# A chain of selective scans on one core: the softplus sum moved to TensorE, and three of sixteen products moved to GpSimd

## The chip, the core and the metric

The kernel runs on one core of a Trainium2 chip. The metric is the device time of one execution in microseconds, the median of several runs. Engines are named as in the profile: PE (TensorE), DVE (VectorE), ACT (ScalarE), POOL (GpSimd), and SP, which issues all the DMA.

## The reference

Four images of 64 x 64 positions with 96 channels pass through four layers. Layer 0 has a gated recurrence; layers 1 to 3 have a two-dimensional selective scan. Every layer ends in a feed-forward block with quantized operands. In layers 1 to 3 the image is normalised, projected to 192 inner channels and a gate z, convolved 3 x 3, and scanned in four orders (rows, columns, each forward and backward), with 16 states per channel. Cut to what matters, from the reference:

```python
dt = jax.nn.softplus(delta + delta_bias[None, :, None])
dA = jnp.exp(dt4[..., None] * A4[None, :, :, None, :])
dBu = dt4[..., None] * u4[..., None] * Bt[:, :, None, :, :]
def step(h, ab):
    a, b = ab
    h = a * h + b
    return (h, h)
_, hs = jax.lax.scan(step, h0, (dA_l, dBu_l))
y = jnp.einsum('lbkdn,lbkn->lbkd', hs, C_l)
return y + u * Dskip[None, :, None]
```

B and C are rows over positions for each state n, the same for all channels. The four orders are added, normalised, multiplied by silu(z) and projected back.

## The kernel before

Layer 0 runs first (`gated`). Then `scans` goes through 12 stages: 4 images for each of layers 1, 2 and 3. A stage has 24 items: 2 directions x 4 segments of T = 1024 positions x 3 chunks of 128 (channel, order) pairs. An item has 16 tiles, one for each state n. That makes 4608 tiles of 128 partitions x 1024 positions in fp32.

For one tile the work is:

- `c_rows`: two DMAs spread the row of C over 64 partitions each, from a scratch tensor `cs` in DRAM (4 buffers).
- `decays`: ACT computes da = exp(delta x decay), into SBUF (3 buffers).
- `b_rows`: PE spreads the row of B over the partitions with a selection matrix `sel`, two bf16 matmuls of 512 columns into a PSUM tile `bc` (2 buffers).
- `scan`: DVE multiplies bc by du = delta x u in place, then runs the scan h = da h + bc.
- `carry`: ACT copies the last column of h for the next segment.
- `times_c`: POOL multiplies h by the rows of C, in place (h has 4 buffers).
- `accumulate`: PE adds h into a PSUM accumulator with four fp32 quarter matmuls. fp32 matmuls are two instructions each in the trace.

The order is written by hand, and each engine works strictly in the order in which its instructions are written (`InOrder`). The loop over k writes, in step k: `carry(k-1)`, `c_rows(k+2)`, `decays(k+2)`, `b_rows(k+1)`, `scan(k)`, `times_c(k-1)`, then side work, then `accumulate(k-2)`.

Side work is written as generators (`Chain`), each `yield` being a point at which the loop takes over again; `pump` advances a chain to its next yield. `yield True` asks for a free PSUM bank, of which side work has two. There are three kinds:

- `prepare_chunk` makes delta and du for the next item. Softplus is computed as max(x, 0) + log(1 + e) with e = exp(-|x|), plus a correction term for the rounding of 1 + e. ACT computes the terms, and POOL adds them in three passes over 128 x 1024. It is pumped once a step and drained at n = 13. Its Ln needs an ACT table other than that of Exp; `logarithms()` uses the visit for the pending norms, and is called once more at n = 11.
- `next_segment` loads u and projects it to the rows of B, C and delta.
- `Job(between(...))` is everything between two layers of another image: joining the four orders, the output projection (`mixer_out`), the feed-forward block, then normalisation, the input projection and the convolution (`convolve`) for the next layer. `Job.step` pumps all its chains `rate` times a step: 1.4, and 1.9 for the last layer's ends. At step 356 of a stage what is left of the job is finished at once. The last image's end runs after the last scan.

All instructions are recorded by one helper, so the profile puts them all on line L80; tiles tell them apart. In the profile `bc` is the row of B or the product, `h` the state, `da` the decay, `c` the row of C, `cs` the scratch with C, `acc` the accumulator, `e`, `delta` and `du` the softplus and its products.

Of the kernel before, what the change touches and what calls it, by code (L numbers as in the profile page):

```python
# [34 lines left out]


CHUNKS = (((0, 0), (64, 1)), ((0, 1), (64, 0)), ((128, 0), (128, 1)))
# [3 lines left out]
NC3 = 48  # L41
XPW = NB3 + 2 * R + NC3
# [59 lines left out]
def metaformer(ctx: ExitStack, tc: tile.TileContext, x, l0_ab, l0_rest, ssm, ffn, out):  # L102
# [58 lines left out]
    stacked = const("stacked", [128, 64])  # L161
    dve.tensor_copy(stacked[0:64], ident[0:64, 0:64])
    dve.tensor_copy(stacked[64:128], ident[64:128, 64:128])
    twice = const("twice", [128, 128])
    dve.tensor_copy(twice[:, 0:64], stacked)
    dve.tensor_copy(twice[:, 64:128], stacked)
# [5 lines left out]
    sel = const("sel", [NB3, NS, 192], BF16)  # L172
    for n in range(NS):
        for k in range(3):
            at = NS * (k % 2) + n
            dve.tensor_copy(
                sel[:, n, 64 * k : 64 * k + 64], mod32[:, at : at + 1].to_broadcast([NB3, 64])
            )
# [7 lines left out]
    minus = const("minus", [128, 1])  # L186
    pool.memset(minus, -1.0)
# [21 lines left out]
    def moments(src, width):  # L209

        st = sb(5, "st", [128, G, 6])
        mv = sb(5, "mv", [128, G, 2])
        for g in range(G):
            dve.bn_stats(st[:, g, :], src[:, g, 0:width])
        for g in range(G):
            dve.bn_aggr(mv[:, g, :], st[:, g, :])
        return mv

    class Norm:
# [7 lines left out]
        def measure(self, src, width, e):  # L227

            mv = moments(src, width)
            yield  # L230
            act.activation(self.v, mv[:, :, 1], AF.Identity, bias=small[e])
            act.activation(self.nm, mv[:, :, 0], AF.Copy, scale=-1.0)
            pending.append(self)

        def settle(self):

            act.activation(self.r, self.r, AF.Exp, scale=-0.5)
            yield
            refine(self.r, self.v)
            pool.tensor_tensor(self.nm, self.nm, self.r, ALU.mult)  # L240

# [76 lines left out]
    def join_orders(im, s, hold):  # L318

        yr, yc = hold["in"].pop(s)  # L320
        if s + 1 < NSTRIP:
            load_y(im, s + 1, hold)
        cols_a, part_c = hold["cols"]
        yt = sb(2, "yt", [128, G, DI])

        def join(ps, g):

            t0, r0 = 128 * g, SR * s + 2 * g
            o, hi = ps[:, g % 2, 0:128], ps[:, g % 2, 128:DI]
            pe.matmul(o, yr[:, t0 : t0 + 128], ident, start=True, stop=False)  # L330
            for r in range(2):
                v = cols_a.rearrange("p (c r) -> p r c", r=HW)[:, r0 + r, :]
                pe.matmul(o[64 * r : 64 * r + 64], v, ident, start=False, stop=True)
            yield
            pe.matmul(hi, yc[:, t0 : t0 + 128], ident[0:64, 0:64], start=True, stop=False)
            for r in range(2):
                for k in range(2):
                    p = slice(64 * k, 64 * k + 64)
                    v = part_c.rearrange("p (c r) -> p r c", r=HW)[p, r0 + r, :]
                    q = 64 * r + 32 * k  # L340
                    pe.matmul(
                        hi[q : q + 32], v, ident[p, p], start=False, stop=True, tile_position=(64 * k, q)
                    )

        for pair in range(2):
            ps = bank("y_t")[:, 0 : 2 * DI].rearrange("p (g c) -> p g c", g=2)
            yield from join(ps, 2 * pair)
            yield
            yield from join(ps, 2 * pair + 1)
            yield  # L350
            act.copy(yt[:, 2 * pair : 2 * pair + 2, :], ps)
            release()
            yield pair == 0
        norm = Norm()
        yield from norm.measure(yt, DI, 1e-5)
        hold["y", s] = yt, norm

    def mixer_out(im, layer, s, hold):
# [6 lines left out]
        normalise(yt, yt, DI, norm.r, norm.nm)  # L365
        yield True
        g = []
        for i, (a, b, z) in enumerate(((0, 128, zl), (128, 192, zh))):
# [12 lines left out]
            for v, z, m in ((g[0], zl, 128), (g[1], zh, 64)):  # L381
                pool.tensor_tensor(v[0:m], v[0:m], z[0:m], ALU.mult)
                yield m == 64
        ps = bank("out_proj")
        for q in range(G):
# [4 lines left out]
            yield  # L390
        x1 = sb(2, "x1", [128, G, C])
# [12 lines left out]
    def load_y(im, s, hold):  # L404
# [4 lines left out]
        sp.dma_start(out=yr[64:128], in_=im.y[1, 64:128, t])  # L409
# [18 lines left out]
    def feed_forward(im, layer, s, hold, dst):  # L428
# [6 lines left out]
        normalise(xh, x1, C, norm.r, norm.nm)  # L435
        yield True
        ps = bank("ff_xt")
        transpose_strip(ps, xh, 0, C)
        yield
# [18 lines left out]
        pool.tensor_copy(hq[:, 2, :], late, saturate=False)  # L458
        yield True
# [16 lines left out]
        for g in range(G):  # L476
            pool.tensor_tensor(y[:, g, :], y[:, g, :], b[:, 3 : 3 + C], ALU.add)
        yield
        x2 = sb(1, "x2", [128, G, C])
        pool.tensor_tensor(x2, x1, y, ALU.add)  # L480
        yield
        sp.dma_start(out=tokens(dst, s), in_=x2)
        if layer < 3:
            norm = hold["norm", s] = Norm()
            yield from norm.measure(x2, C, 1e-6)
# [74 lines left out]
    def convolve(im, layer, s, hold):  # L560
# [10 lines left out]
        for i, group in enumerate(groups):  # L571
# [8 lines left out]
            raw.append(v)  # L580
        for i, v in enumerate(raw):
            act.activation(v, v, AF.Silu, bias=w[:, W_CB + i : W_CB + i + 1])
# [6 lines left out]
        sp.dma_start(out=im.u[1, 64:128, t], in_=raw[0][64:128])  # L589
# [12 lines left out]
        if s == NSTRIP - 1:  # L602
            yield
            sp.dma_start(out=im.u[1, 0:64, :], in_=cols_a[0:64])
# [7 lines left out]
    def between(im, layer, dst=None):  # L612
# [8 lines left out]
        def first():  # L621
            if layer:
                cols_a, part_c = hold["cols"] = columns()
                sp.dma_start(out=cols_a[0:64], in_=im.y[1, 0:64, :])
# [6 lines left out]
                load_y(im, 0, hold)  # L631
            yield
# [70 lines left out]
    class Job:  # L703
# [7 lines left out]
        def step(self):  # L711
            self.credit = min(self.credit + self.rate, 2.0)
# [33 lines left out]
    def load_segment(item):  # L746
# [8 lines left out]
        sg.cs = dram.tile([NC3, T], F32, tag="cs", name="cs")  # L755
        return sg

    def prepare_segment(item, sg):
# [38 lines left out]
        for k in range(2):  # L797
# [3 lines left out]
            yield from project(ps, m, m + NC3, k)  # L801
            act.copy(sg.rows[0:NC3, cols], ps[0:NC3])
            release()
        sp.dma_start(out=sg.cs, in_=sg.rows[0:NC3])

    def prepare_chunk(item):
# [7 lines left out]
        e = sb(1, "e", [128, T])  # L814
        delta, du = sb(2, "delta", [128, T]), sb(2, "du", [128, T])
        for k in range(2):
            cols = slice(k * MM, (k + 1) * MM)
            ps = bank("dt_proj")
            pe.matmul(ps, f, sg.rows[NB3 : NB3 + 2 * R, cols], start=True, stop=True)
            yield  # L820
            act.activation(e[:, cols], ps, AF.Abs, bias=bias)
            act.activation(delta[:, cols], ps, AF.Relu, bias=bias)
            release()
            yield k == 0
        act.activation(e, e, AF.Exp, scale=-1.0)
        act.activation(du, e, AF.Ln, bias=ones)
        logarithms()
        yield
        pool.tensor_tensor(delta, delta, du, ALU.add)
        yield  # L830
        act.activation(du, e, AF.Identity, bias=ones)
        act.activation(du, du, AF.Identity, bias=minus)
        yield
        yield
        pool.tensor_tensor(e, e, du, ALU.subtract)
        yield
        yield
        yield
        pool.tensor_tensor(delta, delta, e, ALU.add)
        yield  # L840
        yield
# [13 lines left out]
    def scans(stages, jobs, pac):  # L855
# [15 lines left out]
        tiles = [(i, n) for i in items for n in range(NS)]  # L871
        live = {}
# [3 lines left out]
        def c_rows(k):  # L876
            i, n = tiles[k]
            c = live[k, "c"] = sb(4, "c", [128, T])
            for half in range(2):
                row = NS * (CHUNKS[i.chunk][0][1] + half) + n  # L880
                sp.dma_start(
                    out=c[64 * half : 64 * half + 64],
                    in_=i.sg.cs[row : row + 1, :].to_broadcast([64, T]),
                )

        def decays(k):
            i, n = tiles[k]
            da = live[k, "da"] = sb(3, "da", [128, T])
# [3 lines left out]
        def b_rows(k):  # L892
            i, n = tiles[k]
            b = live[k, "b"] = wide()
            swap = CHUNKS[i.chunk][0][1]
            for half in range(2):
                cols = slice(half * MM, (half + 1) * MM)
                pe.matmul(
                    b[:, cols], sel[:, n, 64 * swap : 64 * swap + 128], i.sg.bs[:, cols], start=True, stop=True
                )  # L900

        def scan(k):
# [6 lines left out]
            dve.tensor_tensor(b, i.du, b, ALU.mult)  # L909
# [60 lines left out]
        last = len(tiles) - 1  # L970
        chain = segment = None
        c_rows(0)
# [13 lines left out]
        for k in range(last + 4):  # L986
            q, n = divmod(k, NS)
            if k <= last:
# [16 lines left out]
                if n == 11:  # L1005
                    logarithms()
# [3 lines left out]
            if 0 <= k - 1 <= last:  # L1010
                carry(k - 1)
            if k + 2 <= last:
                c_rows(k + 2)
                decays(k + 2)
            if k + 1 <= last:
                b_rows(k + 1)
            if k <= last:
                scan(k)
            if 0 <= k - 1 <= last:
                times_c(k - 1)  # L1020
            if k >= 3 and (k - 3) % NS == NS - 1:
                store(items[(k - 3) // NS])
            if k <= last:
                pump(chain)
                pump(segment)
                if n == 13:
# [3 lines left out]
                work()  # L1030
            if 0 <= k - 2 <= last:
# [240 lines left out]
    for at in range(len(stages)):  # L1272
        jobs.append([])
        if at + 1 < len(stages):
            im, layer = stages[at + 1]
            jobs[-1].append(Job(between(im, layer - 1), 1.4))

        for im in {10: images[:2], 11: images[2:3]}.get(at, ()):
            jobs[-1].append(Job(between(im, 3, im.dst), 1.9))
# [42 lines left out]
def _scan(in_w, conv_w, conv_b, xp_w, dt_w, dt_b, A_logs, Ds, ln_w, ln_b, out_w):  # L1322
# [5 lines left out]
    for d in range(2):  # L1328
        for chunk, halves in enumerate(CHUNKS):
            for k, (ch, order) in enumerate(halves):  # L1330
# [5 lines left out]
                for s in range(3):  # L1336
                    if s % 2 == order:
                        v[:, m + NS * s : m + NS * s + NS] = t[:, R + NS :]
# [69 lines left out]
```

## Time and profile before

| | us |
|---|---|
| runs | 20164.85, 20133.44, 20149.6 (median 20149.6) |
| profiled execution, device time | 20152.58 |
| its span | 20150.8 |
| layer 0 and start, from the windows view | 0 to 1901 |
| the scans of layers 1 to 3 | 1901 to 19692 |
| end of the last image | 19692 to 20151 |
| DVE busy | 17808.5 |
| PE busy | 16417.6 |
| POOL busy | 15531.3 |
| ACT busy | 12295.0 |

An engine's busy time is the union of its instructions; a "mean ns of one" is the duration of one instruction, and neighbours can overlap by some tens of nanoseconds. "Idle before" sums the time in which the engine stood still just before instructions of the group, and names what ended most of it. Matmuls are pipelined and their ends are modelled. The granted clock of PE is given as a share of full speed.

### The profile page before, as it was taken

To read this page: it belongs to the slowest core of one execution; us is meant where nothing else is said; L and a number is where in the kernel's file an instruction comes from. 1 tells how busy PE (TensorE), PEld (TensorE's weight loads), DVE (VectorE), ACT (ScalarE), POOL (GpSimd) and SP (SyncE) were. 2 spreads that over 40 slices of the span, in tenths; PEclk is the share of its full clock that TensorE was granted. 3 is DMA by queue.
4 is the path that set the end of the run, shared out by engine and by line. 5 is a ranking of instruction groups with operands and counts; after the bars stand their busy time and mean duration, and the time that the engine had idled before them with its cause. 6 is when DMAs were issued, how large, how long until landed. Compare 5 with 4: busy or idle time off the path is not lost. (4 is left out here: it accounts for less than half of the span.)

```text
span 20150.8 us, 220842 instructions
## 1 busy us (share of the span) xinstructions
PE 16417.6 (81%) x70656; PEld 4838.3 (24%) x70656; DVE 17808.5 (88%) x13848; ACT 12295.0 (61%) x19373; POOL 15531.3 (77%) x10470
## 2 busy tenths in 40 slices
PE   8998788787888787788788888788788888887776
PEld 3332121121122222222222222222222222222223
DVE  6665999999999998999999999989999999999881
ACT  4444665665665665665665666666666666666553
POOL 3434888888888887888888888878888888878882
PEclk9898796786887797897887887887887887888775
DMA  0002666666666666666666676666676666676661
GB/s 20 16 18 69 165 181 174 166 186 167 168 184 171 164 179 175 166 182 180 167 187 171 167 189 167 169 180 169 170 187 171 168 187 168 170 188 161 172 169 44
DMA packets 1234532, 3148.68 MB, mean 156 GB/s; under 512 B 428049, under 2 KB 428177, under 8 KB 1227217
## 3 DMA queue, kind: packets, MB, share of 16 engines
q1 hardware_dynamic: 1233360, 3134.55, 58.6%
q8 instruction: 554, 9.08, 0.2%
q14 instruction: 618, 5.05, 0.1%
HBM read 2819.18 MB, written 314.57 MB: 156 GB/s over the span
## 5 line engine op out<-in xcount | busy, mean ns | idle before, releaser
L80 POOL TENSOR_TENSOR h<-h,c 128x1024 f32<-128x1024 f32 x4608 | 10834.6, 2358 | 2827.5 <-ACT carry L80 1727.5
L80 DVE TENSOR_TENSOR_SCAN h<-da,carry,bc 128x1024 f32<-128x1024 f32 x4608 | 10814.5, 2347 | 608.7 <-POOL carry L80 10.3
L80 PE MATMUL acc<-h,stacked 64*64 64x512 f32 x36864 | 6179.1, 747 | 498.7 <-POOL h L80 493.8
L80 ACT ACTIVATE da<-delta,decay 128x1024 f32<-128x1024 f32 x4608 | 5280.9, 1147 | 1648.9 <-DVE h L80 1601.8
L80 DVE TENSOR_TENSOR bc<-du,bc 128x1024 f32<-128x1024 f32 x4608 | 5574.5, 1210 | 611.2 <-PE bc L80 586.0
L80 PE MATMUL bc<-bs,sel 96*128 96x512 bf16 x9216 | 3346.9, 451 | 2071.8 <-DVE h L80 2054.6
L80 ACT COPY carry<-h 128x1 f32<-128x1 f32 x3456 | 649.0, 188 | 3533.7 <-DVE h L80 3529.1
L80 PEld LDWEIGHTS <-sel 96*128 96x128 bf16 x9216 | 551.3, 101 | 6988.6 <-DVE h L80 5085.7
L80 PEld LDWEIGHTS acc<-h,stacked 64*64 64x64 f32 x36864 | 1132.5, 153 | 3286.5 <-issue 1699.7
L80 ACT ACT_TABLE_LOAD x1133 | 1453.6, 1283 | 41.6 <-DVE mv L80 22.5
L80 POOL TENSOR_TENSOR c<-h,c 128x512 f32<-128x512 f32 x384 | 485.7, 1265 | 970.5 <-ACT c L80 614.8
L80 PE MATMUL conv<-pad,tap_lo 128*128 128x512 f32 x1728 | 917.5, 630 | 0.0
L80 PE MATMUL dt_proj<-rows,w 12*128 12x512 f32 x1152 | 828.0, 805 | 0.0
L80 ACT ACTIVATE du<-e,ones 128x1024 f32<-128x1024 f32 x576 | 660.8, 1147 | 228.8 <-POOL delta L80 223.2
L80 PE MATMUL x_proj_b<-u,xp 128*108 128x512 f32 x1152 | 671.9, 699 | 94.3 <-DMA xp<-in_ssm 59.0
L80 ACT ACTIVATE c<-c,l_bias 128x512 f32<-128x512 f32 x384 | 263.5, 686 | 753.0 <-PE c L80 737.9
L80 POOL TENSOR_TENSOR delta<-delta,du 128x1024 f32<-128x1024 f32 x288 | 679.5, 2359 | 12.1 <-ACT du L80 12.1
L80 POOL TENSOR_TENSOR e<-e,du 128x1024 f32<-128x1024 f32 x288 | 679.4, 2359 | 2.4 <-ACT du L80 2.4
L80 POOL TENSOR_TENSOR du<-delta,u 128x1024 f32<-128x1024 f32 x288 | 679.4, 2359 | 0.7
L80 POOL TENSOR_TENSOR delta<-delta,e 128x1024 f32<-128x1024 f32 x288 | 678.5, 2356 | 0.1
L80 PE MATMUL x_proj_c<-u,xp 128*48 128x512 f32 x1152 | 624.3, 655 | 64.3 <-ACT rows L80 64.3
L80 PE MATMUL conv<-pad,tap_hi 128*128 128x512 f32 (+1 forms) x1152 | 638.5, 650 | 8.2 <-ACT u L80 8.2
(155 smaller groups left out, 16118.3 us busy)
## 6 DMA issues: line engine op xcount, KB each, us to landing
c<-cs SPq DMA_DIRECT2D x9216, 256.0 KB, 4.1
u<-u SPq DMA_DIRECT2D x288, 512.0 KB, 7.6
y<-y SPq DMA_DIRECT2D x1152, 128.0 KB, 2.4
y<-y SPq DMA_DIRECT2D x144, 512.0 KB, 5.6
xr<-x SPq DMA_DIRECT2D x224, 192.0 KB, 4.8
u<-u SPq DMA_DIRECT2D x288, 128.0 KB, 4.4
pad<-y SPq DMA_DIRECT2D x288, 128.0 KB, 4.6
z<-zl SPq DMA_DIRECT2D x96, 256.0 KB, 2.0
```

The source lines that it names most:

```text
L80: ins = f(*a, **k).ins
```

## The change

The change has four parts.

1. In `prepare_chunk` softplus is computed half by half (512 columns). ACT makes the four terms, PE adds them in PSUM with four fp32 matmuls by the identity, and ACT copies the sum to delta. The three POOL passes go. The call of `logarithms()` at n = 11 goes.
2. The states 2, 7 and 12 (`ON_POOL`) get their product with B on POOL: two DMAs bring the row of B into an SBUF tile `b` (1 buffer) four steps ahead, POOL multiplies it by du two steps ahead, and DVE runs the scan alone. Their decay goes to one of the two PSUM tiles that the rows of B use, one step ahead instead of two. Their rows of B are stored with C in `cs`.
3. Side work is pumped between the product and the scan of a step instead of after `times_c`, `prepare_chunk` gets a second pump at n = 1, 5, 9 and 13, and many chains get more yields between a step and the one that uses its result. Rates rise to 1.8 and 2.6. The silu of the convolution waits for a step whose second next tile isn't a moved one.
4. The halves of the second chunk are swapped, so that `sel` is smaller and all chunks use one layout; four small additions in `feed_forward` become one.

The core of the diff, without the added yields and the swap:

```diff
+CHUNKS = (((0, 0), (64, 1)), ((64, 0), (0, 1)), ((128, 0), (128, 1)))
+ON_POOL = (2, 7, 12)
...
+            both = sb(1, "e", [128, T])
+            e, rest, log, top = both[:, 0:MM], both[:, MM:T], du[:, cols], delta[:, cols]
...
+            act.activation(e, e, AF.Exp, scale=-1.0)
+            act.activation(log, e, AF.Ln, bias=ones)
+            logarithms()
+            yield
+            act.activation(rest, e, AF.Identity, bias=ones)
+            act.activation(rest, rest, AF.Identity, bias=ones, scale=-1.0)
+            yield True
+            ps = bank("delta")
+            for i, v in enumerate((e, rest, log, top)):
+                pe.matmul(ps, ident, v, start=i == 0, stop=i == 3)
+                if i % 2:
+                    yield
+            act.copy(delta[:, cols], ps)
...
-        pool.tensor_tensor(delta, delta, du, ALU.add)
...
-        pool.tensor_tensor(e, e, du, ALU.subtract)
...
-        pool.tensor_tensor(delta, delta, e, ALU.add)
...
+        def pool_rows(k):
+            i, n = tiles[k]
+            b = live[k, "b"] = sb(1, "b", [128, T])
+            from_rows(i, b, NS + ON_POOL.index(n))
+
+        def times_b(k):
+            i, b = tiles[k][0], live[k, "b"]
+            pool.tensor_tensor(b, i.du, b, ALU.mult)
...
+            da = live[k, "da"] = wide() if on_pool(k) else sb(3, "da", [128, T])
...
+            if not on_pool(k):
+                dve.tensor_tensor(b, i.du, b, ALU.mult)
+            beside()
...
+            def beside():
                 pump(chain)
                 pump(segment)
+                if n % 4 == 1:
+                    pump(chain)
                 if n == 13:
                     drain(chain, work)
                     if item.chunk == 2:
                         drain(segment, work)
                 work()
+            if 0 <= k - 1 <= last:
+                carry(k - 1)
+            if on_pool(k + 1):
+                decays(k + 1)
+            if k + 2 <= last:
+                c_rows(k + 2)
+                if not on_pool(k + 2):
+                    decays(k + 2)
+            if on_pool(k + 4):
+                pool_rows(k + 4)
+            if k + 1 <= last and not on_pool(k + 1):
+                b_rows(k + 1)
+            if 0 <= k - 1 <= last:
+                times_c(k - 1)
+            if on_pool(k + 2):
+                times_b(k + 2)
...
+                scan(k, beside)
...
-            jobs[-1].append(Job(between(im, layer - 1), 1.4))
+            jobs[-1].append(Job(between(im, layer - 1), 1.8))
```

## The prediction

> **What bounds the kernel now.** I read first the page's shares by engine and its costliest groups, then the busy time by stage, then who waited for whom inside the scan stage, then the timeline of single tiles. From the page (engine, operation, tiles, count | busy us, mean ns | idle just before, releaser):
>
> ```profile
> PE 16417.6 (81%) x70656; PEld 4838.3 (24%) x70656; DVE 17808.5 (88%) x13848; ACT 12295.0 (61%) x19373; POOL 15531.3 (77%) x10470
> ...
> L80 POOL TENSOR_TENSOR h<-h,c 128x1024 f32<-128x1024 f32 x4608 | 10834.6, 2358 | 2827.5 <-ACT carry L80 1727.5
> L80 DVE TENSOR_TENSOR_SCAN h<-da,carry,bc 128x1024 f32<-128x1024 f32 x4608 | 10814.5, 2347 | 608.7 <-POOL carry L80 10.3
> ...
> L80 DVE TENSOR_TENSOR bc<-du,bc 128x1024 f32<-128x1024 f32 x4608 | 5574.5, 1210 | 611.2 <-PE bc L80 586.0
> ...
> L80 ACT ACT_TABLE_LOAD x1133 | 1453.6, 1283 | 41.6 <-DVE mv L80 22.5
> ...
> L80 POOL TENSOR_TENSOR delta<-delta,du 128x1024 f32<-128x1024 f32 x288 | 679.5, 2359 | 12.1 <-ACT du L80 12.1
> ```
>
> The scans of layers 1 to 3 run from 1901 to 19692 us. The windows view of that stage (us, then busy us of PE, PEld, DVE, ACT, POOL, granted clock, DMA share, GB/s):
>
> ```profile
> 1901.00:19692.00 17791.00, 14439.66 (x64938) 3986.25 (x64930) 16540.16 (x11838) 11257.85 (x17220) 14714.40 (x8979) 0.81 0.65 174
> ```
>
> DVE is the bound: busy 93%. Of its 1251 us idle, 608 us are 132 ns between each product and its scan; 642 us are real waits, nearly all the product waiting for PE's rows of B (586 us). The timeline shows what a tile costs undisturbed (start us, length us):
>
> ```profile
> 10000.50 2.35 DVE L80 TENSOR_TENSOR_SCAN h<-da,carry,bc 128x1024 f32<-128x1024 f32 x1
> ...
> 10002.76 1.21 DVE L80 TENSOR_TENSOR bc<-du,bc 128x1024 f32<-128x1024 f32 x1
> ...
> 10004.11 2.35 DVE L80 TENSOR_TENSOR_SCAN h<-da,carry,bc 128x1024 f32<-128x1024 f32 x1
> ```
>
> Scan to scan is 3.61 us, and 3604 ns is the median over all 4608 tiles. 4608 x 3.604 = 16,607 us; DVE's side work (statistics, residual adds, remainders) adds 542, the waits 642: 17,791. Outside this stage lie 1901 + 459 us of span and 1.8 us around it: 20,152.6 us for the profiled execution, 3.0 us above the median shown.
>
> **The change, part by part.**
>
> *Product moved (DVE).* 3 of 16 tiles are 864. Each loses 1210 + 132 ns on DVE, its pitch falling from 3604 to 2262 ns: **-1159 us**. The scan then reads b from SBUF and da from PSUM; before it was the reverse, so one operand from each: I keep 2347 ns. No row has this pairing; the two scan shapes (1280 ns for 512 columns in the opening stage, 2347 for 1024) leave 213 ns of fixed cost, and half of that either way bounds it: 92 us.
>
> *Side work between product and scan (DVE).* It can fill the 132 ns: about 900 groups, 0 to -119 us. Often it will itself wait for PE or ACT there: **-40**.
>
> *GpSimd.* It loses three softplus passes an item (288 x 3 x 2359 ns) and gains three products (864 x 2358): zero in sum; its 14,714 us then fill about 87% of a shorter stage. But the place matters: the product for tile k+2 is queued in step k behind times_c(k-1), which waits for scan(k-1) and ACT's carry (0.4 us). It ends 0.4 + 2.36 + 2.36 = 5.1 us after scan(k-1), and scan(k+2) may start after two pitches, 7.2 us (6.9 if a step is short in side work). So 1.9 us of lateness are free. GpSimd's side work (1.27 us for a gate product, 0.61 for a cast, 2.36 for du) exceeds this now and then; what queues behind is times_c, then PE's accumulation. Bounds 0 and 864 x 1 us; I take 0.17 us a tile: **+150**.
>
> *ACT.* An item loses 1044 + 2 x 1147 + 1149 ns of full-width passes, and gains eight half-width ones (about 0.67 us each, the Abs/Relu rows) and two copies (0.57): +2.0 us. Ln is now visited twice an item, each visit two table loads of 1283 ns; the explicit flush at n = 11 goes, so loads rise only from 3.2 to 4 or 5 an item. ACT stays near 75%, but look at one visit now:
>
> ```profile
> 10566.50 1.04 ACT L80 ACTIVATE e<-e 128x1024 f32<-128x1024 f32 x1
> 10567.55 1.28 ACT L80 ACT_TABLE_LOAD   x1
> 10568.85 1.15 ACT L80 ACTIVATE du<-e,ones 128x1024 f32<-128x1024 f32 x1
> 10570.02 1.28 ACT L80 ACT_TABLE_LOAD   x1
> 10571.31 1.15 ACT L80 ACTIVATE da<-delta,decay 128x1024 f32<-128x1024 f32 x1
> ```
>
> It is 4.8 us in a 3.6 us step; the carry behind it is late, then times_c, PE's accumulation, and the next rows of B: at 10577.6 us a pitch of 4.15 follows. By scan starts sorted by state, the pitch after n = 3 averages 4200 ns, of which about 445 are wait: 128 us in all. After the change there are two such visits, the first around n = 1, 2 (with the store's 0.99 us copy and a 2.26 us step), the second around n = 7, 8 (again a short step); PE's sum then waits in order for the last ACT term with the rows of B behind it. Bounds 0 (the added yields absorb it) and 3 us an item (864); I take 0.9 us an item: **+250**. The decay of a moved tile is made one step ahead instead of two, in a PSUM buffer freed by scan(k-1); behind the carry it needs 1.4 of 3.6 us, hidden unless ACT is over 2 us late, which is in these bounds.
>
> *PE.* Gained: 288 x 2 x 4 = 2304 fp32 matmuls of 512 columns, two instructions each. Nearest row: conv with tap_lo, 841.6 us busy for 1584 instructions in this stage, 531 ns each: +2448 us. Lost: 1728 instructions for rows of B at 3343.8/9208 = 363 ns: -627. So PE's busy time goes from 14,440 to 16,261 us, above DVE's own floor of about 15,950. This is the dangerous number. Two rows bear on it, one conv tap at either clock:
>
> ```profile
> 10006.95 1.82 PE L80 MATMUL conv<-pad,tap_lo 128*128 128x512 f32 x2
> ...
> 10016.04 1.02 PE L80 MATMUL conv<-pad,tap_lo 128*128 128x512 f32 x2
> ```
>
> The granted clock in the trace is either 1 or 0.5, 0.81 in the mean here, and it was 0.92 in the convolution stretch of a stage (9987 to 10438 us), where PE is busiest, against 0.73 just after it. Taps back to back start 429 ns apart at full clock; by that, the added work is 1977 us and a busy PE has room. It is tight only in the convolution stretch: side rounds go from 1.4 to 1.8 a step, so per step about 1.2 us of convolution, 1.3 of rows and sums, 0.8 of projections and softplus, 3.3 of 3.45 us. That is some 116 steps in each of 11 stages; 0.15 us each: **+190** (0 to 500).
>
> The Trainium skill (Perfetto Trace Analysis, Identifying the Most-Contended Engine) holds matmul busy time a poor measure, since matmuls are pipelined; by it the 16,261 us bind nothing. By the row alone PE would be the longest engine. The skill (TensorE: Matmul & The Clock Gate, Part 1) says an idle window halves the clock and a busy one restores it; by it the added matmuls raise the mean clock, say to 0.9 (an estimate), and PE's time would be 16,261 x 0.81/0.9 = 14,635 us; with the row's 0.81 kept it stays 16,261. No row settles it.
>
> *Queues and jobs.* SP issues 1728 more 256 KB loads: +453 MB, about 212 GB/s and a DMA share near 0.8 instead of 0.65. They come after the rows of C in SP's order and have about 3.7 us of margin beyond the 4.1 us they take to land; nothing on the path, up to +150 if landing doubles. Added yields are paid by the higher rates (old 1.4 x 18/15 is below 1.8). Convolution strips finish earlier, before the forced finish at step 356, which now stalls the product 18.1, 18.0 and 17.0 us: **-53**. More yields elsewhere move nothing: their cover is DVE's pitch.
>
> Sum: 20,152.6 - 1159 - 40 + 150 + 250 + 190 - 53 = **19,490 us**.
>
> **Rivals.** *All is absorbed:* no new wait, 20,152.6 - 1159 - 119 - 53 = 18,820 to 18,940. For it: POOL and ACT total little more than before. Against: every margin shrinks with the pitch. *PE becomes the bound, still faster:* 16,261 us at the 93% that DVE holds today is 17,485 for the stage, 19,850 in all. For it: 81% busy already, products wait for PE alone. Against: the clock rises with load. *Slower:* the softplus sum blocks PE's queue. It stands before the accumulation and the next rows of B, waits there for ACT's last term, and at half clock its two matmuls take 3.6 us; the rows have some 2.9 us of margin (a pitch, less the 0.6 us that they take). If each of the two visits costs 2.8 us, that is 288 x 5.6 = 1610: 20,152.6 - 1252 + 1610 = 20,510. It decides from 1252/288 = 4.3 us of new wait an item, against 2.2 us of all waits today. For it: today's single visit already shows the chain. Against: at full clock the same two matmuls take half.
>
> **How the numbers follow.** Forecast 0.50, all absorbed 0.12, PE-bound 0.15, slower 0.19, and 0.04 that gains and waits cancel within 0.2%, about what a measurement of this kernel can tell from no change. Faster is 0.50 + 0.12 + 0.15 = 0.77. The range reaches from the absorbed case's upper part, 18,880, to 20,340, below the middle of the slower case; the forecast's own range is 19,000 to 19,900.
>
> **What would show it.** Right: 3744 products on DVE; scan to scan near 2.26 us into a moved tile; mean pitch near 3.71 us; POOL's total unchanged; product waits on PE and scan waits on POOL's b together some 1200 us, against 642; clock above 0.81. Wrong: PE busy over 93% of the stage or clock not above 0.81 (PE-bound); waits of products on PE over 1900 us, bunched after the Ln visits (slower); scans longer than 2.35 us with b in SBUF; DMA landing over 8 us.

## The result, and the profile after

The changed kernel takes **21,415.8 us** (median of four runs, 21,398.0 to 21,433.9) against 20,141.5 for the kernel before beside it (20,123.3 to 20,164.9): a ratio of 1.0632, 95% interval 1.0614 to 1.065. It is slower by 6.3%, 1,076 us above the upper end of the predicted range.

First the page of the changed kernel, with the groups that answer to those shown of before (engine, operation, tiles, count | busy us, mean ns | idle just before, releaser):

```profile
PE 17126.7 (80%) x73536; PEld 5510.9 (26%) x73536; DVE 16771.8 (78%) x12968; ACT 13213.9 (62%) x21486; POOL 15511.0 (72%) x10085
...
L80 DVE TENSOR_TENSOR_SCAN h<-da,carry,bc 128x1024 f32<-128x1024 f32 x3744 | 8772.8, 2343 | 698.8 <-POOL carry L80 321.7
L80 DVE TENSOR_TENSOR bc<-du,bc 128x1024 f32<-128x1024 f32 x3744 | 4539.8, 1213 | 2121.5 <-PE bc L80 2083.2
...
L80 POOL TENSOR_TENSOR b<-du,b 128x1024 f32<-128x1024 f32 x864 | 2071.7, 2398 | 347.9 <-DMA b<-cs 347.1
L80 DVE TENSOR_TENSOR_SCAN h<-bc,carry,b 128x1024 f32<-128x1024 f32 x864 | 2014.7, 2332 | 240.4 <-POOL b L80 133.8
L80 ACT ACT_TABLE_LOAD x1518 | 1947.6, 1283 | 53.7 <-DVE mv L80 21.0
...
L80 PE MATMUL delta<-e,ident 128*128 128x512 f32 x2304 | 1307.0, 683 | 492.6 <-ACT e L80 387.2
```

DVE has lost what it should lose: 17,808.5 - 16,771.8 = 1,037 us of busy time. But the product's idle went from 611 to 2,122 us, the scans' from 609 to 939. The windows view of the scans (us, then busy us of PE, PEld, DVE, ACT, POOL, granted clock, DMA share, GB/s; its bounds, like 1901 and 19692 for the kernel before, lie 11 us late by the profile's own clock, where the scans begin at 1988 and 1890, which changes no length, and the shares by under 0.1%):

```profile
1999.00:21070.00 19071.00, 15192.40 (x68121) 4707.96 (x68119) 15517.63 (x11030) 12211.19 (x19414) 14735.41 (x8724) 0.86 0.75 186
```

The stage grew from 17,791 to 19,071 us, and no engine fills it any more: DVE 81% (it was 93%), PE 80%, POOL 77%, ACT 64%. Engines wait for each other. The two waits lists, first PE's and then DVE's (engine, tile, waited for: us in total, times, longest us):

```profile
PE acc L80 <- ACT y L80: 950.3, 259, 9.0
PE delta L80 <- ACT e L80: 387.2, 157, 5.4
```

```profile
DVE bc L80 <- PE bc L80: 2083.2, 873, 32.7
DVE h L80 <- POOL carry L80: 321.7, 72, 11.1
...
DVE h L80 <- POOL b L80: 134.8, 86, 5.6
```

For the kernel before, the first of these lines says

```profile
PE acc L80 <- ACT y L80: 67.3, 72, 5.0
```

So PE's accumulation now waits 950 us for ACT's copy of the finished accumulator (`y`), almost once an item. Sorted by state n from the start times of the trace, in ns an item (mean over 288 items), DVE's idle time just before each kind of work shows where:

| | before | after |
|---|---|---|
| product, all n: us in the stage | 588 | 2089 |
| product at n = 4 | 421 | 3845 |
| product at n = 11 | 19 | 1208 |
| scan at n = 0 | about 132 | 1181 |
| side work, all n: us in the stage | 43 | 514 |

Of 2,089 us, n = 4 has 288 x 3.845 = 1,107. The timeline of one such place (start us, length us, in brackets the idle before and its releaser):

```profile
11216.38 2.35 DVE L80 TENSOR_TENSOR_SCAN h<-da,carry,bc 128x1024 f32<-128x1024 f32 x1
...
11218.45 0.62 ACT L80 ACTIVATE e<-e 128x512 f32<-128x512 f32 x1
11218.64 2.33 DVE L80 TENSOR_TENSOR_SCAN h<-bc,carry,b 128x1024 f32<-128x1024 f32 x1
...
11219.15 1.28 ACT L80 ACT_TABLE_LOAD   x1
11220.44 0.72 ACT L80 ACTIVATE du<-e,ones 128x512 f32<-128x512 f32 x1
...
11221.64 1.28 ACT L80 ACT_TABLE_LOAD   x1
11222.19 2.35 DVE L80 TENSOR_TENSOR_SCAN h<-da,carry,bc 128x1024 f32<-128x1024 f32 x1
11222.93 1.15 ACT L80 ACTIVATE da<-delta,decay 128x1024 f32<-128x1024 f32 x1
11223.99 0.99 ACT L80 COPY y<-acc 128x1024 f32<-128x1024 f32 x1
...
11225.03 1.99 PE L80 MATMUL acc<-y,twice 64*64 64x512 f32 x8 [5.64 <-ACT y L80]
...
11226.80 1.93 PE L80 MATMUL acc<-h,twice 64*64 64x512 f32 x8
...
11228.66 0.79 PE L80 MATMUL bc<-bs,sel 96*128 96x512 bf16 x2
...
11229.49 1.23 DVE L80 TENSOR_TENSOR bc<-du,bc 128x1024 f32<-128x1024 f32 x1 [4.95 <-PE bc L80]
```

To be read from the end: the product of tile 4 waits 4.95 us for its rows of B (11228.66). They stand in PE's queue behind two accumulations, of which the first waited 5.64 us for ACT's copy (11223.99). The copy belongs to step 2, whose scan is the short one at 11218.64, but it runs beside the scan of tile 3, since ACT first went through Exp, a table load, Ln, another load and the decay. There is one accumulator, so PE's first term of the next item must wait for the copy out of it.

The order of the program explains it. The store's copy is written in step 2. Before, `prepare_chunk` took both halves through their first terms before it came to Exp and Ln, so its Ln was written in step 4's side work, two steps behind the copy (265 of 287 items in the trace). In the timeline of before from which the prediction shows a visit at 10566.50, the copy stands 7.2 us ahead of it:

```profile
10559.29 0.99 ACT L80 COPY y<-acc 128x1024 f32<-128x1024 f32 x1
```

Half by half, Exp and Ln of the first half come two steps earlier, and with the second pump at n = 1 they are written in step 1, ahead of the copy (257 of 287 items). The moved tile 2 also makes step 2 shorter by 1.3 us.

### The profile page after: what moved, and what is told of

The parts are those of the page before. It is cut to its first block, busy times and chain, and to the rows that moved or that the text cites. A ratio compares the mean times of both kernels' runs of the same rounds, so it can differ in the third digit from the quotient of the medians.

```text
span 21414.6 us, 231547 instructions
## 1 busy us (share of the span) xinstructions
PE 17126.7 (80%) x73536; PEld 5510.9 (26%) x73536; DVE 16771.8 (78%) x12968; ACT 13213.9 (62%) x21486; POOL 15511.0 (72%) x10085
## 5 line engine op out<-in xcount | busy, mean ns | idle before, releaser
L80 DVE TENSOR_TENSOR_SCAN h<-da,carry,bc 128x1024 f32<-128x1024 f32 x3744 | 8772.8, 2343 | 698.8 <-POOL carry L80 321.7
L80 DVE TENSOR_TENSOR bc<-du,bc 128x1024 f32<-128x1024 f32 x3744 | 4539.8, 1213 | 2121.5 <-PE bc L80 2083.2
L80 PE MATMUL acc<-h,twice 64*64 64x512 f32 x36864 | 5653.2, 692 | 351.6 <-POOL h L80 347.4
L80 ACT ACTIVATE da<-delta,decay 128x1024 f32<-128x1024 f32 x3744 | 4270.7, 1144 | 452.3 <-DVE h L80 445.0
L80 POOL TENSOR_TENSOR b<-du,b 128x1024 f32<-128x1024 f32 x864 | 2071.7, 2398 | 347.9 <-DMA b<-cs 347.1
L80 DVE TENSOR_TENSOR_SCAN h<-bc,carry,b 128x1024 f32<-128x1024 f32 x864 | 2014.7, 2332 | 240.4 <-POOL b L80 133.8
L80 PEld LDWEIGHTS acc<-h,twice 64*64 64x64 f32 x36864 | 1110.4, 145 | 3319.5 <-issue 1901.9
L80 PE MATMUL delta<-e,ident 128*128 128x512 f32 x2304 | 1307.0, 683 | 492.6 <-ACT e L80 387.2
L80 ACT ACTIVATE bc<-delta,decay 128x1024 f32<-128x1024 f32 x864 | 962.8, 1114 | 438.3 <-DVE h L80 390.7
L80 ACT ACTIVATE e<-e,ones 128x512 f32<-128x512 f32 x1152 | 826.6, 718 | 18.7
```

The lines of the kernel that those rows point to most:

```text
L80: ins = f(*a, **k).ins
```

## The experiments

Theory **A**: the delay comes from the order, the first Ln visit ahead of the copy. Rival **B**: it comes from PE's load; then taking out half of the 2304 added matmuls would return their whole duration, 988 us (1152 x 2 instructions, 429 ns apart at full clock in the trace of before). Times are medians; the ratio in brackets is to the kernel before beside it, which took 20,137 to 20,144 us in all four groups.

**Pump later.** Edit to the changed kernel:

```diff
-                if n % 4 == 1:
+                if n in (5, 11):
                     pump(chain)
```

> The second pump of the softplus chain comes at n = 5 and 11 instead of 1, 5, 9, 13, so that the first Ln visit lies in step 2, behind ACT's copy of the finished accumulator, and the second at n = 8. Theory A (late copy: the first Ln visit stands on ACT ahead of the copy y<-acc, PE's first accumulation of the next item waits for that copy, and the rows of B for tile 4 queue behind it): the product's wait at n = 4, now 3.85 us an item, falls under 1 us, some of it comes back one or two steps later; 20,300 to 20,600 us. Theory B (PE load: the 2304 added fp32 matmuls fill PE): no matmul goes, so 21,300 to 21,500 us, the waits only move.

Measured: 20,554.6 us (1.021, 1.0193 to 1.0227), 861 less. The product's wait at n = 4 falls from 3,845 to 722 ns, at n = 11 from 1,208 to 72.

```profile
PE acc L80 <- ACT y L80: 143.8, 115, 3.6
```

With the same work and the same matmuls, the turn of a few yields returns two thirds of the loss. This is A. But the edit moves the second half of softplus as well; so one more run takes away the pump at n = 1 alone.

```diff
-                if n % 4 == 1:
+                if n in (5, 9, 13):
```

> The changed kernel with one thing undone: no second pump of the softplus chain at n = 1 (it stays at n = 5, 9 and 13). The first Ln visit then falls into step 2, behind the accumulator's copy. Late-copy theory: 20,500 to 20,650 us, as in the first experiment (20,555), and PE's wait for the copy (950 us) under 250. If the other moved pumps made that gain: over 21,000 us.

Measured: 20,910.7 us (1.0381, 1.0366 to 1.0395), 505 less, between the two. PE's waits of this kernel:

```profile
PE delta L80 <- ACT e L80: 592.9, 260, 7.6
...
PE acc L80 <- ACT y L80: 148.4, 122, 2.9
```

The wait for the copy is gone as fully as in the run above, and the product's wait at n = 4 is down to 793 ns, so the late copy is worth 505 us, net of waits that grew elsewhere. The other 356 go mostly with the second sum: PE stands before ACT's last terms (593 us here, 109 in the run above), and the wait at n = 11 stays at 1,150 ns. That is the chain of the prediction's slower rival; it had set 288 x 2.8 = 806 us for each visit.

**Copy first.** The copy is written at the head of step 2:

```diff
             step["n"] = n
+            if k >= 3 and (k - 3) % NS == NS - 1:
+                copy_y(items[(k - 3) // NS])
             if 0 <= k - 1 <= last:
```

> ACT's copy of the finished accumulator is written first in step 2, ahead of the carry and the decay with its table load; the Ln visit stays in step 1. Theory A: the copy comes 0.19 + 1.28 + 1.14 = 2.6 us earlier, so PE's wait for it (950 us in all) and the product's wait at n = 4 fall by about two thirds: 20,700 to 20,900 us. Theory B: 21,350 to 21,450 us.

Measured: 21,040.3 us (1.0446, 1.0431 to 1.0462), 375 less; right in direction, smaller than expected. PE's wait for the copy halves to 468.5 us, and the wait at n = 4 goes to 2,054 ns: the visit of step 1 is still ahead.

**Half the matmuls.** PE sums only the log term and the maximum; the correction for the rounding of 1 + e is left out:

```diff
-            for i, v in enumerate((e, rest, log, top)):
-                pe.matmul(ps, ident, v, start=i == 0, stop=i == 3)
-                if i % 2:
-                    yield
+            for i, v in enumerate((log, top)):
+                pe.matmul(ps, ident, v, start=i == 0, stop=i == 1)
+                yield
```

> PE sums two of the four softplus terms (log and max; the correction for the rounding of 1 + e is left out), so 1152 fp32 matmuls of 512 columns go; ACT still makes all four terms. Theory B: PE is freed of 1152 x 0.86 = 988 us, and that comes off: about 20,430 us. Theory A: the wait at n = 4 stays at 3.8 us an item; only PE's wait for the ACT terms at n = 9 and 10 (483 us on PE, 348 us of product wait at n = 11) can go: 21,000 to 21,250 us.

Measured: 20,967.5 us (1.0412, 1.0397 to 1.0428), 448 less. The wait at n = 4 is untouched (3,844 ns; PE for the copy 939.5 us); at n = 11 it goes to 121, since the sum no longer takes ACT's two last terms. The time lies a little below A's range and far above B's: load is not the main cause. It may have a part in these 448 us, which this run does not separate from the wait for ACT's terms.

**The carry zeroed earlier.** For the first segment POOL zeroes a tile of carries. `scan` writes that. Before, `scan` stood ahead of `times_c`; the changed order puts `times_c` and `times_b` ahead of `scan`, and so of the clearing. The edit:

```diff
+            if k <= last and n == 0 and item.first:
+                carries[item.chunk] = sb(2, f"carry{item.chunk}", [128, NS])
+                pool.memset(carries[item.chunk], 0.0)
             if 0 <= k - 1 <= last:
```

> The clearing of a chain's carry is written at the head of its first step, ahead of times_c and times_b on POOL's queue, as it effectively was before. Both theories: the scan's wait at n = 0 falls from 1181 to about 200 ns an item (72 waits of 4.5 us on POOL's carry, 322 us): 21,090 to 21,150 us. If DVE only waits for something else there, 21,300 to 21,400 us.

Measured: 21,167.7 us (1.0511, 1.0496 to 1.0527), 248 less; the scan's wait at n = 0 falls from 1,181 to 175 ns. A second loss, independent of the first: both mends together,

> The later visit and the early clearing together, with the three moved states: the schedule of the run without moved states (20,430 us). If the two effects add: 20,555 - 248 = 20,307 us, so the moved products are worth only about 120 of their 1159 us. If they are worth more than half: under 19,900 us.

gave 20,271.1 us (1.0063, 1.005 to 1.0077), 284 below the later pump alone. That returns 1,145 of the 1,274 us with all 2304 matmuls in place. But DVE has 1,159 us less to do than before, and the kernel is still not faster. The rest of the runs ask why.

**No moved tile**, otherwise as the last one; all products stay on DVE:

```diff
-ON_POOL = (2, 7, 12)
+ON_POOL = ()
```

> No state is moved (the list is empty); the softplus sum on PE, the later visit of the first experiment and the early clearing of the carry stay. If the moved products are worth their 1159 us of DVE time and cost some waits (the scan's waits at n = 2, 7, 12, about 430 us, and a shorter pitch for everything else): DVE's floor is 16,607 + 549 us again, with some 1000 us of waits, 20,450 to 20,600 us, which is slower than the same schedule with the moved products (about 20,300 by the two single effects). If the moved products are what costs: under 20,150 us.

Measured: 20,430.2 us (1.0145, 1.013 to 1.016), just under the expected range. So on an equal schedule the moved products bring 20,430 - 20,271 = 159 us, of 1,159 removed. The two windows, without moved tiles and with them:

```profile
1994.00:20153.00 18159.00, 15546.20 (x69954) 4767.80 (x69946) 16503.74 (x11915) 12292.19 (x19467) 12773.24 (x7895) 0.88 0.65 170
```

```profile
1996.00:19981.00 17985.00, 15207.61 (x68228) 4652.09 (x68220) 15518.18 (x11050) 12212.48 (x19467) 14738.68 (x8758) 0.87 0.79 197
```

DVE falls from 91% to 86% of the stage, while POOL rises from 70% to 82%. And without moved tiles the rest of the change costs 1.45% by itself: its DVE waits in the stage show 716 us for rows of B (586 before) and 209 us `rows <- ACT bs`, which is not among that stage's longer waits before. All of DVE's waits before side work come to 379 us (43 before); side work now stands between product and scan.

**Moved products alone**, with the softplus of before on POOL, one visit and no second pump (and the carry zeroed early):

```diff
-            for i, v in enumerate((e, rest, log, top)):
...
+        pool.tensor_tensor(delta, delta, du, ALU.add)
...
+        pool.tensor_tensor(e, e, du, ALU.subtract)
...
+        pool.tensor_tensor(delta, delta, e, ALU.add)
...
-                if n % 4 == 1:
-                    pump(chain)
```

> The moved products with the softplus of before: three POOL passes, one Ln visit at n = 2 behind the accumulator's copy, one pump a step, the flush at n = 11; the carry cleared early. POOL's busy time rises to 14,714 + 864 x 2.36 = 16,750 us, so POOL, not PE, is the longest engine. Late-copy theory: no wait at n = 4 over 0.7 us; the product of b comes late in POOL's queue; 19,900 to 20,400 us. PE-load theory: 2304 matmuls fewer, so well under 20,000 us with PE's busy time near 13,850 us.

Measured: 21,180.7 us (1.0517, 1.0501 to 1.0532), a miss by 780 us. The Ln visit lay in step 4, as before the change, and not at n = 2; the product's wait at n = 4 is 1,657 ns, where none over 0.7 us was expected. Its window of the scans:

```profile
1984.00:20906.00 18922.00, 14379.85 (x63642) 4013.56 (x63634) 15543.55 (x11050) 11330.34 (x17425) 16685.53 (x9619) 0.79 0.74 187
```

Its line of PE's waits for POOL's h, and below it that of the kernel before:

```profile
PE acc L80 <- POOL h L80: 1783.9, 1182, 11.1
```

```profile
PE acc L80 <- POOL h L80: 493.8, 375, 5.3
```

POOL is at 88%, not full, and yet PE's accumulation waits 1,784 us for it. Here a queue in order at 88% is late often enough to hold up the next. That this is what costs most in this kernel is read from the waits and not tested by a run.

**Side work behind the scan.** From the kernel with both mends, `beside()` goes from ahead of the scan to behind it:

```diff
-            beside()
             h = live[k, "h"] = sb(4, "h", [128, T])
...
+            beside()
```

> As the last one, with side work behind the scan again. DVE's side work then has a whole scan more before it is read: its waits fall from about 540 us to 170 us, while the gap between product and scan goes back to 132 ns (some 60 us): 20,000 to 20,150 us if those waits stood on the bound, 20,250 to 20,330 us if they only move to the products.

Measured: 20,211.5 us (1.0032, 1.002 to 1.0043), 60 less, between the two expectations. DVE's waits before side work fall from 571 to 167 us, but most of that moves to other waits; at n = 12 the scan waits 1,052 ns.

**All mends.** In addition POOL's product with B comes ahead of `times_c`, and its rows of B are asked for ahead of the rows of C (`pool_rows` ahead of `c_rows`, not shown):

```diff
-            if 0 <= k - 1 <= last:
-                times_c(k - 1)
             if on_pool(k + 2):
                 times_b(k + 2)
+            if 0 <= k - 1 <= last:
+                times_c(k - 1)
```

> Four mends together: the later visit, the early clearing, side work behind the scan again instead of between product and scan, and on POOL the product with b ahead of times_c, with the rows of b issued ahead of the rows of C. From 20,555 us: 248 less for the clearing, 100 to 250 for DVE side work that waited in front of a scan (541 us of such waits now against 43 before), 100 to 250 for the scan's waits at n = 2, 7, 12: 19,850 to 20,100 us. If PE's load is the bound, nothing below 20,250.

Measured: 20,172.9 us (1.0017, 1.0008 to 1.0027), above the expected range; 39 less than the last one, but its runs overlap with those of the last one (20,150.6 to 20,203.3 against 20,191.0 to 20,216.6). DVE's waits for POOL's product fall from 299 to 66 us, and PE's for POOL's h rise from 632 us to:

```profile
PE acc L80 <- POOL h L80: 825.2, 573, 13.7
```

The wait has changed its place. Four edits to this kernel then look for what holds it.

*One visit.* Exp and Ln full-width, once an item, with the correction made in place between PE's first and last two matmuls:

```diff
+        act.activation(e, e, AF.Exp, scale=-1.0)
+        act.activation(du, e, AF.Ln, bias=ones)
+        logarithms()
...
+            pe.matmul(ps, ident, e[:, cols], start=True, stop=False)
+            pe.matmul(ps, ident, du[:, cols], start=False, stop=False)
```

> As the mended kernel, but with one full-width Exp and Ln an item, at n = 4, and the correction term made in place between PE's first and last two matmuls; the flush at n = 11 is back and there is no extra pump. Table loads fall from about 1520 to 1150 (475 us of ACT). If ACT's visits are what makes PE and POOL late: 100 to 300 us under the mended kernel, 19,650 to 19,950 us. If PE's matmuls are: no difference, since all 2304 stay.

Measured: 20,249.0 us (1.0054, 1.0039 to 1.0069). Table loads fall from 1,520 to 1,143, and the time does not fall: a miss. The run does not price the loads, because the order of the side work changed with them, and other waits grew: the product's at n = 4 from 541 to 2,015 ns and at n = 9 from 178 to 1,059. What makes them grow was not followed up.

*Half the matmuls* (the same edit as above, now on this kernel):

> The mended kernel (20,173 us) with two of the four softplus terms summed on PE, the correction for the rounding of 1 + e left out: 1152 fp32 matmuls fewer. If PE's load is what still eats the 1159 us that DVE gained: 988 us come off PE and most of them off the time, 19,300 to 19,500 us. If POOL's and ACT's lateness does, with PE only passing it on in its fixed order: 20,000 to 20,150 us.

Measured: 19,851.5 us (0.9854, 0.9841 to 0.9868): 321 us for 988 us of PE's work by the expectation's price, between the two theories. PE's busy time fell by 792 us, from 17,170 to 16,378, at a lower mean clock.

*No du on POOL*:

```diff
-        pool.tensor_tensor(du, delta, sg.us[item.chunk], ALU.mult)
```

> The mended kernel without POOL's pass du = delta x u (the logarithm's term stands in for du): 288 x 2.36 = 680 us less on POOL, nothing less on PE or ACT. If POOL's lateness still eats the gain (PE's accumulation waits 827 us for POOL's h, and rows of B queue behind it): 19,780 to 19,920 us. If PE's load does: 20,120 to 20,180 us.

Measured: 19,963.8 us (0.9912, 0.9898 to 0.9925): 209 us for 680 us of POOL's work, a little above the range expected for POOL's lateness, and PE's waits for POOL's h fall from 825 to 542 us.

*One more step between ACT's terms and PE's sum*:

```diff
+            yield
             yield True
...
-                if n in (5, 11):
+                if n in (5, 7, 11, 12):
```

> The mended kernel with one more step between ACT's last softplus term and PE's sum (a yield more, pumps at n = 5, 7, 11, 12). PE's wait for the ACT terms (316 us) goes and the product's waits at n = 4 to 6 and 11 shrink: 19,930 to 20,080 us if PE's order passes ACT's lateness on; 20,130 to 20,200 us if those waits only move.

Measured: 20,285.7 us (1.0069, 1.0056 to 1.0082), 113 more: a miss. The sum waits less for ACT's term `e` (32 us instead of 120), but the product waits more at n = 13 (1,082 ns instead of 830) and n = 14 (777 instead of 142). That the added pumps pack too much into single steps is a reading that no run tests.

So neither PE nor POOL is the one bound: taking 988 us from the one or 680 from the other returns about a third of it. What is left looks like lateness shared between queues that run at 68 to 87% of the stage. In the kernel with all mends POOL also waits 1,570 us for ACT's carry and 436 for its rows of B from DRAM (259 in the kernel with the first two mends), and no run takes either wait away. Which single hand-over costs most was not settled.

**Two moved tiles** in the kernel with all mends:

```diff
-ON_POOL = (2, 7, 12)
+ON_POOL = (6, 13)
```

> The mended kernel with two moved states, 6 and 13, instead of 2, 7 and 12. DVE has 288 x 1.342 = 386 us more, POOL 679 us less. If the waits of short steps and of POOL's queue are worth about as much as DVE's gain, 20,100 to 20,300 us; if DVE's time still counts in full, 20,500 us or more.

Measured: 20,116.5 us (0.9982, 0.9973 to 0.9991). It does all of the work and is faster than both kernels, though than the one before by 0.18% only, about what a measurement can tell. With the copy written first in addition (the same edit as above),

> The version with two moved states (20,116 us), with the accumulator's copy written first in its step. PE's wait for that copy there is 132 us; half of it or more goes: 20,030 to 20,110 us, faster than both kernels. If the carry behind the copy makes POOL late instead: 20,110 to 20,200 us.

it is 20,166.2 us (1.0013, 1.0004 to 1.0022), 50 more, though PE's wait for the copy falls from 132 to 38 us. With the visit out of the way the copy held PE up little, and the carry now stands behind its 0.99 us. That the carry is what costs the 50 us was not run by itself.

## Why the prediction was wrong, point by point

- **Products removed, -1159: right as an amount of work.** 864 products are gone; the pitch of a moved tile has a median of 2,264 ns (2,262 predicted), and the scan with b in SBUF and the decay in PSUM takes 2,332 ns, against 2,343 for the others; the bound of 92 us was not needed. Wrong as a gain: the sum took all 1,159 us off the time, and on an equal schedule they bought 159. Even with all mends the kernel stays at 20,173 us, some 680 above the forecast of 19,490; which waits make up that remainder stays open.
- **ACT, +250, bounds 0 and 3 us an item: the step that failed.** It names the store's 0.99 us copy, but only as a length on ACT. It left out who waits for it: PE's first accumulation, with the rows of B behind, 950 us in all (67 before). The wait at n = 4 alone grew from 0.42 to 3.85 us an item, beyond the bound for both visits. Taking the n = 1 pump away returned 505 us, moving the other pumps 356.
- **POOL, +150: near in size for the wait it names, short in scope.** Scans waited 134.8 us for POOL's b. But the carry's memset was passed by two POOL instructions in the same edit, and the prediction did not list it among the steps moved: 322 us of wait, 248 when mended alone. The 347 us that POOL waits for the rows of B from DRAM were not foreseen either, nor sized by a run.
- **Side work between product and scan, -40; "More yields elsewhere move nothing": wrong in sum.** Side work fills some of the 132 ns: without moved tiles the idle time just before the scans is 517 us, against 609 before the change. But it also waits there itself, in front of the scan, 514 us in the changed kernel instead of 43, and the prediction set no price on that. Moving it behind returned 60.
- **PE, +190, and the PE-bound rival: load was not the bound, but not this cheap.** Leaving out half of the sum's matmuls returned 321 us in the kernel with all mends. The prediction had 16,261 us at an unchanged clock, or 14,635 at 0.9; measured are 15,192 us, 80% of the stage, at 0.86. The Trainium skill (TensorE: Matmul & The Clock Gate, Part 1) says a busy window restores the clock; the trace agrees in direction, 0.81 before and 0.86 after, and 0.79 in the kernel with moved products and no sum on PE.
- **The slower rival: right queue, wrong item first.** PE's queue with the rows of B behind did decide, and at the first visit; what it waited for was mostly the copy (950 us), less ACT's last term (387).
- **Forced finish, -53: wrong.** The three long pitches of before (20.6, 21.6 and 21.8 us, at steps 356 and 360) became 36.3, 21.7 and 22.2 at steps 359 and 360, and five more stages have one of 15 to 16 us at step 360.
- **DMA: right in bytes, wrong in margin.** 3,598 MB were moved instead of 3,149, at a share of 0.75 in the stage. The rows of B were to have 3.7 us of margin; POOL waited for them before 218 of 864 products.
- **"Today's single visit already shows the chain": not shown by the place it names.** The pitch of 4.15 us that the prediction set at 10577.6 us came from raw start times, which run 10.9 us ahead of the profile's; it begins at 10566.66, beside the visit. The product there waits 0.44 us behind an accumulation that had waited 3.02 us for POOL's h, and POOL had waited 7.11 us for a row of C from DRAM. Those two waits were over by 10566.61, just as the visit began.

The ledger from the changed kernel: 21,416 - 505 (n = 1 pump) - 356 (the other pumps) - 284 (carry) = 20,271; - 60 (side work behind the scan) - 39 (b first, not separable from no change) = 20,173.

## What to carry to other kernels

When an instruction is moved on an in-order engine, write down what it now stands ahead of, and for each of those who waits, down to the bound engine: here one pump put some 3.9 us of ACT work (Exp, Ln and two table loads, between 11218.45 and 11222.93 in the timeline) ahead of a 1 us copy, and the loss appeared two queues away, as DVE waiting for PE. Work removed from the bound engine can be worth far less than its duration: here 1,159 us off DVE bought 159, with the other engines between 68 and 85% of the stage and waiting for each other. A setup instruction that is written inside a moved block, such as a memset, moves with it.

## What the runs showed of the hardware

The mean granted clock of PE in the scan stage rose with PE's work: 0.79 and 0.81 without the sum on PE (14,380 and 14,440 us busy), 0.84 and 0.85 with half of it (14,470 and 14,480), 0.86 to 0.89 with all of it (15,150 to 15,550). With it the matmuls that were already there became shorter: those of `acc<-h` took 768 ns each at 0.79, 747 at 0.81 and 692 at 0.86. GpSimd's product of 128 x 1024 fp32 took 2,374 to 2,398 ns with its operands in SBUF, against 1,213 on DVE with one in PSUM, and the DVE scans beside it were no longer than before (2,331 to 2,347 ns).
